# First attention layer of a two-layer graph network: an order written out by hand on all engines, with fixed distances

## The chip, the cores and the metric

The kernel runs on one core of a Trainium2 chip. The core has five engines, each with its own queue that is worked through in order: TensorE (PE; its weight loads are shown apart as PEld), VectorE (DVE), ScalarE (ACT), GpSimd (POOL) and SyncE (SP). In this kernel POOL issues the gathers from device memory and SP issues nearly all other transfers. The metric is the time of one execution on the device in microseconds (us), lower is better. Of the kernel before there are 25 timed executions (median 4665.8, from 4651.89 to 4680.75) and one profiled execution of 4664.45.

## The reference

There are 6250 nodes with 256 features each and 100,000 edges, sorted by destination; each edge has one of 6 types. A node's row is normalized, and then two attention layers follow. The change is in the first. Cut to what matters there:

```python
k_rel = einsum('nhd,rhde->rnhe', k, rel_att)      # 4 heads of 64
v_rel = einsum('nhd,rhde->rnhe', v, rel_msg)
key_e = k_rel[edge_type, edge_src]
val_e = v_rel[edge_type, edge_src]
att = (q[edge_dst] * key_e).sum(-1) * rel_pri[edge_type] / sqrt(64)
seg = edge_dst * 6 + edge_type
ex = exp(att - segment_max(att, seg)[seg])
w = ex / segment_sum(ex, seg)[seg]
hsum = segment_sum(w[:, :, None] * val_e, seg)
```

So each edge needs a gathered row (its key and its value, 512 floats), a dot product per head with the query of its destination, a softmax over the edges with the same destination and type, and a weighted sum of values into its destination.

## The kernel before, in words

An earlier part of the kernel sorts the edges by (destination, type), computes all queries into an SBUF tile `QA` (one block of 126 nodes after another) and all keys and values into a table `kv_d` in device memory. The second layer and two stages over the nodes come later and are not touched.

The first attention layer works on 832 tiles of 128 edges, in 26 chunks of 32 tiles (`C` = 32, `NC` = 26). For a tile `t` it does this:

- **Gather** (line 642, POOL): the 128 rows of key and value go into a ring of 12 lanes with 6 slots each (lines 665 to 679). `gather_more` issues the gather of tile `t` only when tile `t - 12` has been scored and tile `t - 60` has been weighed.
- **Expand q** (lines 724 to 750): SP fetches the row numbers of 4 tiles (`near`), DVE makes one-hot matrices of them (`nbe`), and PE multiplies the one-hots with a block of `QA`. The result for two tiles, `qe`, lies in PSUM with two buffers. The block number is loaded into registers of PE, 8 tiles at a time.
- **Score** (lines 753 and 756, DVE): multiply `qe` with the gathered keys (`pr`), and reduce to 4 numbers per edge (`att`). Two tiles go through one instruction.
- **Softmax over the chunk** (`chain`, from line 763 to 868): a serial string of some 20 steps that passes between PE (transposes), ACT (copies, exponentials) and DVE (forward and backward scans): the maximum of each segment first, then the sum. It ends with the weights `wt` (line 862) and, for a segment that goes on from the chunk before, a correction `factor` (line 868).
- **Weigh** (lines 892 and 897, ACT): scale the gathered values with `wt`, four instructions per tile, into `wrows` (two buffers of 4 tiles).
- **Sum** (`one_hots` line 875, product line 960, `add` line 905): DVE makes one-hots `ebn` of 4 tiles, PE multiplies them with `wrows` into `aps` (PSUM, three buffers), and DVE adds `aps` to a block of `QA`. A block's sums lie where the queries of the block before were.
- **Move** (lines 916 to 940): between two chunks the running sum of a segment that goes on is corrected with `factor`, through a product (line 929), `moved` (lines 932 and 938) and an add (line 940).

While chunk `c` is weighed and summed (`bulk(c)`), chunk `c + 1` is scored and its softmax done (`chain(c + 1)`); the loop at the end of the stage interleaves the two generators. The order in which the program is written is not the order of the queues, however. A scheduler of the framework goes over what was written and orders each engine's queue by its own estimate of when an instruction can start. In the queues that it made, the product of one tile often stands between the two products of the next q, two `pr` may come before their two reductions, adds of line 905 stand between the steps of the softmax, and some instructions of the next chunk's scoring stand among the softmax of this one.

Of the kernel before, what the change touches and what calls it, by code (L numbers as in the profile page):

```python
# [17 lines left out]
P = 128  # L18
# [6 lines left out]
def kernel(  # L25
# [81 lines left out]
    def dap(t, offset, ap):  # L107
        a = t[:, :]
        return bass.AP(tensor=a.tensor, offset=a.offset + offset, ap=ap)
# [540 lines left out]
    with ExitStack() as st:  # L650
# [13 lines left out]
        def slot(t):  # L664
            return L - 1 - (t // NL) % L
# [35 lines left out]
        def flat(v, back):  # L701
            v = v.rearrange("p h t -> p (h t)")
            return v[:, ::-1] if back else v

        def chain(c, res):

            keeps = cp.tile([P, 2, P], F32, name="keeps", bufs=2)
# [8 lines left out]
            whole_s = cp.tile([1, 2, H, C], F32, name="whole_s")  # L716
            nc.scalar.activation(whole_s, whole, AF.Exp)
            att = cp.tile([P, H, C], F32, name="att", bufs=2)
            for k in range(0, C, 8):
                t0 = c * C + k  # L720
                oh = []
                for i in range(0, 8, GT):
                    near = op.tile([P, GT, P], BF16, name="near")
                    nc.sync.dma_start(
                        near.rearrange("p g e -> p (g e)"), dap(row_d, (t0 + i) * P, [[0, P], [1, GT * P]])
                    )
                    oh.append(op.tile([P, GT, P], F32, name="nbe"))
                    nc.vector.tensor_scalar(oh[-1], near, ipart, None, op0=OP.is_equal)
                _, bs = nc.values_load_multi_w_load_instructions(
                    blk[0:1, t0 : t0 + 8],  # L730
                    engines=[mybir.EngineType.PE],
                    min_val=0,
                    max_val=NB - 1,
                    skip_runtime_bounds_check_because="blk is at most NB - 1",
                )
                for j in range(0, 8, 2):
                    t = t0 + j
                    qe = pq.tile([P, 2, D], F32, name="qe")
                    for i in range(2):
                        ordered(  # L740
                            nc.tensor.matmul(  # L741
                                qe[:, i, :],
                                oh[j // GT][:, j % GT + i, :],
                                QA[:, 1:, :D][:, bass.ds(bs[j + i], 1), :].rearrange("p a d -> p (a d)"),
                                start=True,
                                stop=True,
                            ),
                            "q",
                            "sums",
                        )  # L750
                    pr = wp.tile([P, 2, H, DK], F32, name="pr")
                    lane = t % NL
                    nc.vector.tensor_tensor(  # L753
                        pr.rearrange("p t h e -> p t (h e)"), ring[:, lane : lane + 2, slot(t), :], qe, op=OP.mult
                    )
                    nc.vector.tensor_reduce(  # L756
                        att[:, :, k + j : k + j + 2].rearrange("p h t -> p t h"), pr, AX.X, OP.add
                    )
                    scored[0] = t + 2
                    gather_more()  # L760
                    yield
            x = pt.tile([P, P], F32, name="turn")
            nc.tensor.transpose(x, att.rearrange("p h t -> p (h t)"), ident)
            yield
# [103 lines left out]
                nc.scalar.activation(factor, fps, AF.Identity, bias=ones[:, 0:1])  # L868
                res["factor"] = factor

        state = {"hot": None, "regs": {}}

        def one_hots(t):
            o = wp.tile([P, GT, P], F32, name="ebn")
            nc.vector.tensor_tensor(
                o,
                ifree[:, None, :].to_broadcast([P, GT, P]),
                dl0[:, t : t + GT, None].to_broadcast([P, GT, P]),
                op=OP.is_equal,
            )  # L880
            return o

        def bulk(c, w, factor):

            wvs, sums = {}, {}
            hot = {}

            def weigh(j):
                t = c * C + j
                if j % GT == 0:  # L890
                    wvs[j // GT] = wp.tile([P, GT, AV], F32, name="wrows")
                    nc.scalar.copy(wvs[j // GT][:, :, D:], start[:, t : t + GT, :])  # L892
                wv = wvs[j // GT]
                v = ring[:, t % NL, slot(t) + 1, :]
                for h in range(H):
                    cols = slice(h * DK, (h + 1) * DK)
                    nc.scalar.activation(wv[:, j % GT, cols], v[:, cols], AF.Copy, scale=w[:, h, j : j + 1])  # L897
                used[0] = t + 1
                gather_more()

            def add(j):
                t = c * C + j
                a = QA[:, bass.ds(state["regs"][t], 1), :].rearrange("p a d -> p (a d)")
                ordered(
                    nc.vector.scalar_tensor_tensor(a, a, same[:, t : t + 1], sums.pop(j), op0=OP.mult, op1=OP.add),  # L905
                    "sums",
                    "q",
                )
                del state["regs"][t]

            weigh(0)
            weigh(1)
            hot[0] = one_hots(c * C)
            if c:
                t = c * C - 1
                _, (at,) = nc.values_load_multi_w_load_instructions(
                    blk[0:1, t : t + 1],
                    engines=[mybir.EngineType.PE, mybir.EngineType.DVE],
                    min_val=0,
                    max_val=NB - 1,  # L920
                    skip_runtime_bounds_check_because="blk is at most NB - 1",
                )
                move = wp.tile([P, P], F32, name="move", bufs=1)
                nc.vector.tensor_scalar(
                    move, ifree, target[:, c : c + 1], top_row, op0=OP.is_equal, op1=OP.mult
                )
                a = QA[:, bass.ds(at, 1), :].rearrange("p a d -> p (a d)")
                ps = pp.tile([P, AV], F32, name="aps")
                nc.tensor.matmul(ps, move, a, start=True, stop=True)
                yield  # L930
                moved = wp.tile([P, AV], F32, name="moved", bufs=1)
                nc.vector.tensor_tensor(
                    moved[:, :D].rearrange("p (h e) -> p h e", h=H),
                    ps[:, :D].rearrange("p (h e) -> p h e", h=H),
                    factor[:, :, None].to_broadcast([P, H, DK]),
                    op=OP.mult,
                )
                nc.scalar.copy(moved[:, D:], ps[:, D:])
                ordered(
                    nc.vector.scalar_tensor_tensor(a, a, keep, moved, op0=OP.mult, op1=OP.add), "sums", "q"  # L940
                )
                yield
            for j in range(C):
                t = c * C + j
                if j % 8 == 0:
                    _, bs = nc.values_load_multi_w_load_instructions(
                        blk[0:1, t : t + 8],
                        engines=[mybir.EngineType.DVE],
                        min_val=0,
                        max_val=NB - 1,  # L950
                        skip_runtime_bounds_check_because="blk is at most NB - 1",
                    )
                    for i in range(8):
                        state["regs"][t + i] = bs[i]
                if j + 2 < C:
                    weigh(j + 2)
                if j % GT == 2 and j + 2 < C:
                    hot[j // GT + 1] = one_hots(t + 2)
                ps = sums[j] = pp.tile([P, AV], F32, name="aps")
                nc.tensor.matmul(  # L960
                    ps, hot[j // GT][:, j % GT, :], wvs[j // GT][:, j % GT, :], start=True, stop=True
                )
                if j % 8 != 0 and j:
                    add(j - 1)
                if j % 8 == 7:
                    add(j)
                yield

        res = {}
        gather_more()  # L970
        for _ in chain(0, res):
            pass
        for c in range(NC):
            todo = bulk(c, res["w"], res.get("factor"))
            ahead = chain(c + 1, res) if c + 1 < NC else iter(())
            for k in range(C // 2):
                next(ahead, None)
                if k in (1, 3) or k % 2 and k > 4:
                    next(todo, None)
            for _ in todo:  # L980
                next(ahead, None)
            for _ in ahead:
                pass

    acc0 = QA[:, :NB, :]
    adst = pers.tile([P, NB, 3, 2 * H], BF16, name="adst")
# [422 lines left out]
```

## Time and profile before

| | us |
|---|---|
| profiled execution, its own time | 4664.45 |
| its span (first to last instruction) | 4662.7 |
| median of 25 timed executions | 4665.8 |
| first `pr` of the first attention layer | 943.4 |
| transposes of the scores (line 763) of chunks 0, 1 and 25 | 993.0, 1041.3, 2628.3 |
| last add of the layer (line 905) | 2683.4 |

The page gives busy time by engine, the span in 40 slices, a chain of waits, and groups of instructions by line. A group's line has its count, its busy time and the mean of one in ns, and after the bar the idle time of its engine just before it with what ended it. "remote" there means that a signal arrived without an instruction or transfer that ended just then; "issue" that nothing shown ended the wait. Timeline rows give start and length in us, the engine, line and operation, how many were merged (x2), and in brackets the idle time before. A length of two merged instructions that is under twice the length of one shows that they overlap: what counts for a sum is the distance of starts. An fp32 product is recorded as two weight loads and two matmuls, so 832 products of a line are x1664.

### The profile page before, as it was taken

How to read it: one execution, taken by the hardware profiler on the slowest of the kernel's cores; microseconds unless marked ns; L12 is line 12 of the kernel's file. 1: busy time of each engine (PE TensorE's matmuls, PEld its weight loads, DVE VectorE, ACT ScalarE, POOL GpSimd, SP SyncE). 2: the span in 40 equal slices, each digit the busy share in tenths (PEclk: the TensorE clock that was granted, in tenths of full speed). 3: DMA queues.
4: the chain of work that ended last, by engine and by line, in shares of the span. 5: the costliest groups of instructions: out<-in, count | busy, mean ns of one | idle time of the engine just before them, and what ended most of it. 6: DMA issues, size and time to landing. Idle time of an engine off the chain costs nothing. (4 is left out here: it accounts for less than half of the span.)

```text
span 4662.7 us, 51896 instructions
## 1 busy us (share of the span) xinstructions
PE 3113.7 (67%) x12464; PEld 2112.4 (45%) x12464; DVE 3049.0 (65%) x7131; ACT 1448.7 (31%) x5577; POOL 1722.9 (37%) x1808
## 2 busy tenths in 40 slices
PE   4996699856676666666666788852566665666672
PEld 3775577634444444444444455531333443344432
DVE  7567211057777777767776788862666666666798
ACT  4332233225554555545544722210100100000102
POOL 0000000064444544454444200025676766676500
PEclk9998899977778887878887988865777777767676
DMA  2334333264445544454454332323333333334423
GB/s 91 122 115 117 84 128 117 104 201 134 140 144 156 160 145 139 133 158 136 132 152 147 68 85 73 72 78 108 100 106 114 111 109 113 107 111 115 82 69 101
DMA packets 265355, 545.35 MB, mean 117 GB/s; under 512 B 66696, under 2 KB 175227, under 8 KB 255483
## 3 DMA queue, kind: packets, MB, share of 16 engines
q0 software_dynamic: 106496, 328.97, 25.2%
q1 hardware_dynamic: 150929, 208.18, 14.6%
q10 hardware_dynamic: 7636, 4.88, 0.4%
q8 instruction: 111, 1.82, 0.2%
q14 instruction: 183, 1.50, 0.1%
HBM read 436.56 MB, written 105.28 MB: 116 GB/s over the span
## 5 line engine op out<-in xcount | busy, mean ns | idle before, releaser
L642 POOL DMA_INDIRECT ring<-kv_d,idx x832 | 811.3, 975 | 947.0 <-ACT wrows L897 425.2
L642 POOL DMA_INDIRECT rows<-xw_d,idx x832 | 871.7, 1048 | 477.2 <-issue 357.0
L1288 PE MATMUL aps<-wrows,ebn 128*128 128x264 f32 x1664 | 665.5, 541 | 290.5 <-DVE acc L1296 164.2
L897 ACT ACTIVATE wrows<-ring,wt 128x64 f32<-128x64 f32 x3328 | 833.7, 335 | 6.1 <-issue 5.9
L960 PE MATMUL aps<-wrows,ebn 128*128 128x258 f32 x1664 | 601.6, 470 | 253.0 <-DVE QA L905 105.5
L741 PE MATMUL qe<-QA,nbe 128*128 x1664 | 537.6, 461 | 212.1 <-DVE pr L753 78.2
L1288 PEld LDWEIGHTS aps<-wrows,ebn 128*128 128x128 f32 x1664 | 384.1, 258 | 507.7 <-issue 229.6
L741 PEld LDWEIGHTS qe<-QA,nbe 128*128 128x128 f32 x1664 | 369.6, 232 | 335.8 <-issue 170.0
L960 PEld LDWEIGHTS aps<-wrows,ebn 128*128 128x128 f32 x1664 | 333.6, 225 | 408.8 <-ACT wrows L897 167.6
L753 DVE TENSOR_TENSOR pr<-ring,qe 128x512 f32<-128x512 f32 x416 | 279.0, 680 | 296.6 <-remote 189.7
L171 POOL MEMSET ntype<- 128x128 int32 x100 | 29.7, 298 | 1148.7 <-DVE hm L186 768.8
L905 DVE SCALAR_TENSOR_TENSOR QA<-QA,same,aps 128x258 f32 x832 | 389.7, 468 | 83.2 <-PE aps L960 48.6
L1296 DVE TENSOR_TENSOR acc<-acc,aps 128x264 f32 x832 | 349.5, 420 | 43.9 <-issue 12.6
L1152 ACT COPY asr<-rows 128x16 f32<-128x16 f32 x208 | 44.8, 218 | 792.2 <-DMA rows<-xw_d,idx 772.2
L1272 DVE TENSOR_TENSOR wrows<-rows,ex 128x1024 f32<-128x1024 f32 x208 | 253.9, 1221 | 47.5 <-PE aps L1288 19.2
L756 DVE TENSOR_REDUCE att<-pr 128x8 f32<-128x512 f32 x416 | 272.4, 678 | 0.6
L892 ACT CAST wrows<-start 128x8 f32<-128x8 bf16 x208 | 39.2, 189 | 606.0 <-remote 232.5
L344 ACT COPY rel<-nps 128x384 f32<-128x384 f32 x400 | 163.2, 493 | 96.3 <-PE nps L343 96.3
L195 PE MATMUL nps<-wa_s,tm 128*128 128x256 f32 x600 | 167.6, 438 | 6.0 <-DVE tm L186 6.0
L1180 DVE TENSOR_TENSOR ad<-ad 128x256 f32<-128x256 f32 x26 | 11.0, 424 | 241.8 <-ACT ad L1177 135.1
L334 PE MATMUL nps<-hm,wv_s 128*128 128x128 f32 x1200 | 160.5, 284 | 0.0
L334 PE MATMUL nps<-hm,wk_s 128*128 128x128 f32 x1200 | 160.5, 284 | 0.0
(368 smaller groups left out, 4503.5 us busy)
## 6 DMA issues: line engine op xcount, KB each, us to landing
kv_d<-rel SPq DMA_DIRECT2D x49, 1512.0 KB
near<-row_d SPq DMA_DIRECT2D x208, 128.0 KB
nbe<-row_d SPq DMA_DIRECT2D x26, 1024.0 KB
ring<-kv_d,idx POOLq DMA_INDIRECT x832
rows<-xw_d,idx POOLq DMA_INDIRECT x832
xbuf<-in_x_dram SPq DMA_DIRECT2D x98, 126.0 KB
xw_d<-xw SPq DMA_DIRECT2D x49, 128.0 KB
xbuf<-xw_d SPq DMA_DIRECT2D x49, 128.0 KB
```

Of the source, the lines that this page charges most:

```text
L195: nc.tensor.matmul(ps, m[:, t, c, :], W[:, t, c, :], start=(t == 0 and c == 0), stop=False)
L334: nc.tensor.matmul(tp[:, o, :], W[:, t, c, cols], m[:, t, c, :], start=(t == 0 and c == 0), stop=False)
L642: nc.gpsimd.indirect_dma_start(out=to, out_offset=None, in_=table[:, :], in_offset=bass.IndirectOffsetOnAxis(ap=index, axis=0))
L741: nc.tensor.matmul(qe[:, i, :], oh[j // GT][:, j % GT + i, :], QA[:, 1:, :D][:, bass.ds(bs[j + i], 1), :].rearrange("p a d -> p (a d)"), s ...
L753: nc.vector.tensor_tensor(pr.rearrange("p t h e -> p t (h e)"), ring[:, lane : lane + 2, slot(t), :], qe, op=OP.mult)
L756: nc.vector.tensor_reduce(att[:, :, k + j : k + j + 2].rearrange("p h t -> p t h"), pr, AX.X, OP.add)
L897: nc.scalar.activation(wv[:, j % GT, cols], v[:, cols], AF.Copy, scale=w[:, h, j : j + 1])
L905: nc.vector.scalar_tensor_tensor(a, a, same[:, t : t + 1], sums.pop(j), op0=OP.mult, op1=OP.add),
L960: nc.tensor.matmul(ps, hot[j // GT][:, j % GT, :], wvs[j // GT][:, j % GT, :], start=True, stop=True)
L1272: nc.vector.tensor_tensor(wv[:, :, :, :DK], rows[:, :, :, :DK], ex[:, 0, mine, :, None].to_broadcast([P, GT, H, DK]), op=OP.mult,)
L1288: nc.tensor.matmul(ps.rearrange("p h e -> p (h e)"), oh[:, j, :], wv[:, j].rearrange("p h e -> p (h e)"), start=True, stop=True,)
L1296: nc.vector.tensor_tensor(a, a, ps, op=OP.add)
```

## The change

The whole layer is now recorded under `manual_schedule`: every engine's queue has its instructions in the order in which they are written, and the scheduler moves nothing there. The order is written anew to that end:

- The row numbers are fetched two groups of 4 tiles ahead (`fetch_rows`), the one-hots for q made one group ahead (`near_one_hots`), the products for q issued one pair of tiles ahead (`expand_q(t + 2)` before `score(t)`), also across a chunk's end.
- The add of a tile comes after the next tile's product, throughout, also across groups of 8 tiles and across a chunk's end (`add(t - 1)` after `multiply(t)`). Before, the adds of the 7th and 8th tile of each group of 8 both came right after the 8th product.
- The one-hots for the sums (`one_hots`) are made after the second tile of a group of 4 for the next group, also across chunks.
- In the loop over a chunk's 16 scored pairs, the first three pairs go with the move (three steps), and each of the other 13 pairs with one tile's sum. The remaining 19 tiles go one by one with the steps of the softmax.
- The softmax of the first chunk is done before any other work of the layer starts.

No instruction is added to or taken from the work on a tile, and no buffer's size is changed. The diff, cut to its core:

```diff
+        def near_one_hots(g):
+            if g < NT // GT:
+                near_hot[g] = op.tile([P, GT, P], F32, name="nbe")
+                nc.vector.tensor_scalar(near_hot[g], nears.pop(g), ipart, None, op0=OP.is_equal)
+                fetch_rows(g + 2)
+
+        def expand_q(t):
...
+            qe = spread[t] = pq.tile([P, 2, D], F32, name="qe")
+            for i in range(2):
+                ordered(
+                    nc.tensor.matmul(
+                        qe[:, i, :],
+                        near_hot[t // GT][:, t % GT + i, :],
+                        QA[:, 1:, :D][:, bass.ds(pe_regs.pop(t + i), 1), :].rearrange("p a d -> p (a d)"),
...
+        def score(t, to):
+            if t % GT == 0:
+                near_one_hots(t // GT + 1)
+            pr = wp.tile([P, 2, H, DK], F32, name="pr")
...
+            scored[0] = t + 2
+            gather_more()
...
         def chain(c, res):
...
-            for k in range(0, C, 8):
...
+            for t in range(c * C, (c + 1) * C, 2):
+                expand_q(t + 2)
+                score(t, att[:, :, t % C : t % C + 2])
+                yield
...
         def bulk(c, w, factor):
...
-            weigh(0)
-            weigh(1)
-            hot[0] = one_hots(c * C)
+            for j in range(2):
+                weigh(c * C + j, w)
             if c:
+                add(c * C - 1)
...
             for j in range(C):
                 t = c * C + j
...
                 if j + 2 < C:
-                    weigh(j + 2)
-                if j % GT == 2 and j + 2 < C:
-                    hot[j // GT + 1] = one_hots(t + 2)
-                ps = sums[j] = pp.tile([P, AV], F32, name="aps")
-                nc.tensor.matmul(
-                    ps, hot[j // GT][:, j % GT, :], wvs[j // GT][:, j % GT, :], start=True, stop=True
-                )
-                if j % 8 != 0 and j:
-                    add(j - 1)
-                if j % 8 == 7:
-                    add(j)
+                    weigh(t + 2, w)
+                if j % GT == 1:
+                    one_hots(t // GT + 1)
+                multiply(t)
+                if j:
+                    add(t - 1)
                 yield
 
         res = {}
-        gather_more()
-        for _ in chain(0, res):
-            pass
-        for c in range(NC):
-            todo = bulk(c, res["w"], res.get("factor"))
-            ahead = chain(c + 1, res) if c + 1 < NC else iter(())
-            for k in range(C // 2):
-                next(ahead, None)
-                if k in (1, 3) or k % 2 and k > 4:
-                    next(todo, None)
-            for _ in todo:
-                next(ahead, None)
-            for _ in ahead:
-                pass
+        with tc.manual_schedule():
+            gather_more()
+            for g in range(2):
+                fetch_rows(g)
+            near_one_hots(0)
+            for g in range(1):
+                one_hots(g)
+            expand_q(0)
+            for _ in chain(0, res):
+                pass
+            for c in range(NC):
+                todo = bulk(c, res["w"], res.get("factor"))
+                ahead = chain(c + 1, res) if c + 1 < NC else iter(())
+                early = 3 if c else 0
+                for k in range(C // 2):
+                    next(ahead, None)
+                    if k < early or k >= 3:
+                        next(todo, None)
+                for _ in todo:
+                    next(ahead, None)
+                for _ in ahead:
+                    pass
+            add(NT - 1)
```

## The prediction

> **What bounds the kernel now.** I read the page first, for the share of this layer; then busy time by stage, cut where the transposes of the scores (line 763) stand; then VectorE's waits in the long stage; then timelines, for what one instruction costs from its start to the next one's.
>
> The page:
>
> ```profile
> span 4662.7 us, 51896 instructions
> L642 POOL DMA_INDIRECT ring<-kv_d,idx x832 | 811.3, 975 | 947.0 <-ACT wrows L897 425.2
> L753 DVE TENSOR_TENSOR pr<-ring,qe 128x512 f32<-128x512 f32 x416 | 279.0, 680 | 296.6 <-remote 189.7
> ```
>
> The sum is made against the profiled execution, 4664.45 (its span and 1.75 around it); the median of 25 is 4665.8, 1.4 above, so nothing is corrected for it. The multiplication with q stood idle longer than it worked, mostly on a signal with no visible releaser.
>
> Busy time by stage (length, then PE, PEld, DVE, ACT, POOL, granted clock, DMA share, GB/s):
>
> ```profile
> 1041.00:2628.00 1587.00, 1036.37 (x3445) 694.97 (x3443) 1174.32 (x2635) 832.29 (x3641) 740.98 (x759) 0.81 0.49 144
> 2628.00:2649.00 21.00, 17.52 (x56) 9.57 (x54) 19.17 (x54) 17.00 (x76) 0.00 (x0) 0.84 0.00 1
> 2649.00:2684.00 35.00, 24.73 (x73) 12.15 (x72) 22.71 (x47) 33.03 (x144) 1.31 (x2) 0.95 0.01 3
> ```
>
> The first row is 24 periods, each with one chunk's sum and the next one's scoring and softmax: 1587 / 24 = 66.1 us. DVE is busy 1174.32 / 24 = 48.9 of that, more than any other engine, and idle 17.2. The second row is the softmax of the last chunk beside sums, with nothing left to gather: DVE is busy 91%. So DVE bounds the layer, and 17.2 us a period are all that a better order can win. What DVE waits for in the first row (total, times, longest):
>
> ```profile
> DVE pr L753 <- remote: 160.3, 36, 8.4
> DVE pr L753 <- PE qe L741: 48.5, 51, 3.6
> DVE QA L905 <- PE aps L960: 37.8, 61, 2.0
> DVE one L774 <- issue: 36.2, 10, 6.2
> DVE pr L753 <- issue: 33.2, 29, 5.7
> DVE QA L905 <- remote: 12.8, 7, 3.2
> ```
>
> Two kinds. In 48.5 + 37.8 = 86.3 us (3.6 a period) PE was really late. In 160.3 + 36.2 + 33.2 + 12.8 = 242.5 us (10.1 a period) PE had ended long before. One such place, PE first, then DVE:
>
> ```profile
> 1477.92 3.39 PE L741 MATMUL qe<-QA,nbe 128*128 x8
> 1488.87 2.08 PE L741 MATMUL qe<-QA,nbe 128*128 x4 [7.13 <-DVE pr L753]
> ```
>
> ```profile
> 1478.08 0.69 DVE L875 TENSOR_TENSOR ebn<-ifree,dl 128x512 f32<-128x512 f32 x1
> 1478.68 0.48 DVE L905 SCALAR_TENSOR_TENSOR QA<-QA,same,aps 128x258 f32 x1
> ...
> 1488.13 0.69 DVE L753 TENSOR_TENSOR pr<-ring,qe 128x512 f32<-128x512 f32 x1 [6.64 <-remote]
> ...
> 1495.35 0.50 DVE L728 TENSOR_SCALAR nbe<-near,ipart 128x512 f32<-128x512 bf16 x1
> 1495.77 1.27 DVE L753 TENSOR_TENSOR pr<-ring,qe 128x512 f32<-128x512 f32 x2
> 1496.96 1.27 DVE L756 TENSOR_REDUCE att<-pr 128x8 f32<-128x512 f32 x2
> 1498.15 0.47 DVE L905 SCALAR_TENSOR_TENSOR QA<-QA,same,aps 128x258 f32 x1
> 1498.54 0.68 DVE L753 TENSOR_TENSOR pr<-ring,qe 128x512 f32<-128x512 f32 x1
> ```
>
> The products for q ended at 1481.3, the `pr` that needs them starts at 1488.13, and then PE too has been idle for 7.13. I call these **held signals**. None appears before the layer's first gather, nor in the second row above, where POOL is idle; I take them to belong to long trains of gathers. What holds them the trace doesn't tell.
>
> **The change, part by part.** The second timeline also gives what an instruction costs in a full queue, start to start: `pr` (1496.96 − 1495.77) / 2 = 0.60, reduction 0.60, add 0.39, `nbe` 0.42 at most (0.40 elsewhere), `ebn` 0.60. No instruction on a tile is added or removed, so the change is worth what it does to the 17.2 idle us.
>
> *First half of a period* (16 pairs scored; the move; 13 tiles summed). On DVE: 16 × (0.60 + 0.60) = 19.2; 8 `nbe` × 0.40 = 3.2; 13 adds × 0.39 = 5.1 (12 of this chunk, one left over); 3 `ebn` × 0.60 = 1.8; `move`, `moved` and the move's add about 1.0 as their busy times; loading block numbers 0.1 (no busy time is shown for it; a gap, by estimate). Sum **30.4**. The others' cover: ACT weighs a tile in 1.0 (33.03 us for 144 instructions, four a tile and some others, in the third row), against 1.9 of DVE per step; PE has a pair for q and one product.
>
> *POOL* gathers the same 832 tiles in the same sequence, a pair 2 × 1.25 = 2.5 (record 0.975, starts 1.25 apart), more than DVE's 1.9. The first half thus eats 16 × 0.6 = 9.6 us, 8 tiles, of the 12 tiles' lead; the softmax half, in which nothing is scored, gives it back. Should the lead run out, `pr` waits for gathers; before, that cost 12.8 us in the whole stage.
>
> *Softmax half* (19 tiles, each beside a step of the softmax). The second row is the same mixture: **21.0**. Bounds: its busy 19.17 below; above, ACT's weighing, 19 × 1.0, and the softmax's own copies and exponentials, 2.5, make 21.5. At its end the next chunk need not wait: the first pair's q is already expanded, and weighing runs two tiles ahead.
>
> *q two tiles ahead, adds one tile behind* (lines 741, 753, 905, 960). These lengthen PE's head start by a step, about 1.9 us, against true lateness of 48.5 / 51 = 1.0 and 37.8 / 61 = 0.6 us a time. I take 1.0 of the 3.6 us a period as left; bounds 0 and 3.6. What is late next is the other direction: `qe` has two PSUM buffers, so the products for pair t + 2 wait on PE for the `pr` of t − 2, and the tile's product for the sum is queued behind them. In steady state that `pr` is a step old; after a DVE stall both catch up together.
>
> *One-hots four tiles ahead* (lines 728, 875). They move to fixed places, same count. `near` is fetched two groups ahead, four steps or some 7.7 us, and in before its one-hots waited for it 1.0 us in the whole stage. Cost 0; without that cover, the 2.4 us in which a gather lands (from POOL's record to its end) bound one such wait, 8 a period at worst.
>
> *SP.* 208 `near` and, per chunk, the loads of `keeps` and `whole` are the same transfers. The latter now stand behind a chunk's last `near`, and `whole` waits for the scans (line 790) of the chunk before, some 5 us into the softmax half. It is needed 25 us later and the next `near` some 15 later: 0, or 2 us a period if it should land late.
>
> *Edge.* The first softmax now stands alone: in before, from 993 to 1014, `pr` of chunk 1 ran between its steps. Of the work moved out, about half filled idle DVE; I take **+6** once (0 to 12). The last chunk is as before.
>
> *Held signals.* They hit whoever waits for PE, and two tiles of distance (about 2 us) do not cover 6.6. The number of gathers per period is the same, so I keep **10.1**. Bounds: 0 (second row: none), and doubled, 20, since the first half is now one unbroken train and a strict order has nothing else to run.
>
> **Sum:** 30.4 + 21.0 + 1.0 + 10.1 = 62.5 a period against 66.1: 24 × 3.6 = 86 less; 4664.45 − 86 + 6 = **4584**. Its own range, with 0 to 3.6 for true lateness, ± 1.5 for the halves: 4540 to 4640.
>
> *A rule that speaks against this.* After idling 7.13 us, PE takes 2.08 for four matmuls, where eight took 3.39, and the granted clock of the stage is 0.81. The Trainium skill ("TensorE: Matmul & The Clock Gate", section "HAM oscillation — how this bites in real kernels") says that PE idling longer than some 3.4 us falls back to half clock. By it, any wait of a strictly ordered PE behind DVE would be paid twice. If PE ran at half clock through the whole first half (8 matmuls in 3.39, so 1.7 per pair, and 1.1 for a tile's product), its step of 2.8 would pass DVE's 1.9: 13 × 0.9 = 12 us a period, and 4872 in all. By the rows, PE idles that long only in a held signal, once or twice a period, and its cost is in the 10.1.
>
> **The rivals.**
>
> *Held signals vanish.* If they came from the particular order in before (matmul after matmul with waits between), the period is 52.4: 24 × 13.7 = 329 less, **4341**. For it: 2628 to 2649 runs so. Against it: that stretch has no gathers. Chance 0.16.
>
> *Held signals grow: slower.* Place: every `pr` of the first half, with PE's product and DVE's add queued behind it. From 66.1 − 52.4 − 0.25 (the edge) = **13.5** us a period on, the change loses. For it: the trains get longer, and when before stalled, adds and softmax steps of other tiles could sometimes run ahead. Against it: in before, too, each queue was fixed once compiled, and `pr` stood at the head of it. At 16 us: 68.4, 24 × 2.3 + 6 = 61 more, 4726; at 20: 24 × 6.3 + 6 = 157 more, 4822. As one number **4740**. Chance 0.28.
>
> *Nothing comes of it:* the removed PE waits return as waits for PSUM or for gathers (the lead of 12 runs out: 2 to 4 us a period). Then 4664 ± 20. Chance 0.12: 0.04 faster, 0.05 same, 0.03 slower.
>
> **How the numbers follow.** The forecast has 0.44. Faster: 0.44 + 0.16 + 0.04 = 0.64; same 0.05; slower 0.28 + 0.03 = 0.31. About 0.2%, 9 us, is what a measurement of this kernel can tell from no change. The range reaches to 4420, leaving out two thirds of the case with no held signals, and to 4745, leaving out four tenths of the slower one (0.11 each, with the tails).
>
> **What would show it.** Right: line 782 of the new kernel (the transposes) 62 to 63 us apart; first halves near 31 plus held time, softmax halves near 21; `pr <- PE qe` and `QA <- PE aps` together under 30 us; "remote" and "issue" still near 240. Wrong: softmax halves of 25 or more (the interleaving is bound by ACT or by a step of the string); `pr <- DMA ring` in tens of us (gather lead too short); "remote" below 100 or above 350 (held signals follow the order, not the gathers).

## The result and the profile after

The changed kernel takes 4729.35 us (median of 7 runs, 4720.96 to 4738.47) against 4665.69 for the kernel before: a ratio of 1.0136, 95% interval 1.0119 to 1.0152. It is slower by 64 us where 82 us of gain were forecast. The profiled execution of the changed kernel took 4723.66, its span is 4721.9.

The page of the changed kernel; the last two lines are groups (count, busy time and mean, and after the bar the idle time before them with what ended most of it):

```profile
span 4721.9 us, 51320 instructions
L642 POOL DMA_INDIRECT ring<-kv_d,idx x832 | 812.9, 977 | 1003.5 <-issue 376.8
L756 DVE TENSOR_TENSOR pr<-ring,qe 128x512 f32<-128x512 f32 x416 | 283.4, 681 | 298.1 <-remote 228.5
```

The idle time before `pr` is what it was (298.1, before 296.6), and more of it is "remote". The transposes of the scores of chunks 1 and 25 (line 782) stand at 1049.5 and 2688.2, so 24 periods take 1639 us, 68.3 each (66.1 before). Busy time by stage; the columns are window, length, then PE, PEld, DVE, ACT, POOL, the granted clock, DMA share and GB/s:

```profile
1049.00:2688.00 1639.00, 1070.88 (x3453) 696.32 (x3452) 1233.71 (x2640) 833.28 (x3648) 742.89 (x759) 0.82 0.47 140
```

DVE now works 51.4 us a period (48.9 before) and is idle 16.9 (17.2 before). What DVE waits for in these 24 periods (total, times, longest):

```profile
DVE pr L756 <- remote: 214.5, 51, 6.9
DVE QA L934 <- PE aps L929: 43.2, 46, 3.5
DVE QA L934 <- issue: 23.7, 14, 3.5
DVE pr L756 <- PE aps L929: 16.5, 12, 2.0
DVE QA L934 <- remote: 14.8, 8, 2.8
DVE pr L756 <- PE qe L738: 14.7, 26, 0.6
DVE QA L934 <- PE qe L738: 12.9, 9, 2.1
DVE pr L756 <- issue: 12.6, 4, 4.0
```

The order did in part what it was meant to do: a `pr` waits 14.7 us for its own products where it had waited 48.5, but an add waits 43.2 us for its product (37.8 before). The four rows of held signals, "remote" and "issue", are 265.6 us (242.5 before; 273.6 if the first and the last chunk are counted too, the number that two expectations below start from), and the four rows of waits for PE are 87.3. A stretch of DVE's timeline in a scored half:

```profile
1495.23 0.47 DVE L934 SCALAR_TENSOR_TENSOR QA<-QA,same,aps 128x258 f32 x1
1495.62 0.68 DVE L756 TENSOR_TENSOR pr<-ring,qe 128x512 f32<-128x512 f32 x1
1496.34 0.69 DVE L759 TENSOR_REDUCE att<-pr 128x8 f32<-128x512 f32 x1
1496.94 0.47 DVE L934 SCALAR_TENSOR_TENSOR QA<-QA,same,aps 128x258 f32 x1
1497.33 0.48 DVE L718 TENSOR_SCALAR nbe<-near,ipart 128x512 f32<-128x512 bf16 x1
1503.90 0.69 DVE L756 TENSOR_TENSOR pr<-ring,qe 128x512 f32<-128x512 f32 x1 [6.09 <-remote]
```

Two things are in it. A step runs as reckoned, about 2 us, until a signal is held for 6.09 (the profile models when a product ends on PE, so it can't tell whether the signal or the end of the product was late). And `pr` to its own reduction is 1496.34 − 1495.62 = 0.72, not 0.60; the reduction reads what `pr` has just written. By halves, averaged over 24 periods: the softmax half, transposes to `wt`, takes 22.3 (reckoned 21.0), the scored half 45.9 (reckoned 30.4 and the held time).

### The profile page after: what moved, and what is told of

It is laid out like the page before. It is cut to its first block, busy times and chain, and to the rows that moved or that the text cites. A ratio compares the mean times of both kernels' runs of the same rounds, so it can differ in the third digit from the quotient of the medians.

```text
span 4721.9 us, 51320 instructions
## 1 busy us (share of the span) xinstructions
PE 3152.1 (67%) x12464; PEld 2116.5 (45%) x12464; DVE 3111.3 (66%) x7131; ACT 1447.9 (31%) x5577; POOL 1728.0 (37%) x1808
## 5 line engine op out<-in xcount | busy, mean ns | idle before, releaser
L1313 PE MATMUL aps<-wrows,ebn 128*128 128x264 f32 x1664 | 676.4, 549 | 282.6 <-DVE acc L1321 176.1
L738 PE MATMUL qe<-QA,nbe 128*128 x1664 | 571.6, 483 | 374.2 <-DVE pr L756 247.2
L929 PE MATMUL aps<-wrows,ebn 128*128 128x258 f32 x1664 | 586.4, 452 | 76.6 <-issue 26.7
L756 DVE TENSOR_TENSOR pr<-ring,qe 128x512 f32<-128x512 f32 x416 | 283.4, 681 | 298.1 <-remote 228.5
L934 DVE SCALAR_TENSOR_TENSOR QA<-QA,same,aps 128x258 f32 x832 | 394.2, 474 | 128.2 <-PE aps L929 54.3
L759 DVE TENSOR_REDUCE att<-pr 128x8 f32<-128x512 f32 x416 | 286.1, 688 | 14.4
L1193 PE MATMUL ad<-adst,nbe 128*128 x832 | 102.6, 179 | 92.6 <-issue 82.2
```

The costliest lines, as they stand in the source:

```text
L738: nc.tensor.matmul(qe[:, i, :], near_hot[t // GT][:, t % GT + i, :], QA[:, 1:, :D][:, bass.ds(pe_regs.pop(t + i), 1), :].rearrange("p a d ...
L756: nc.vector.tensor_tensor(pr.rearrange("p t h e -> p t (h e)"), ring[:, lane : lane + 2, slot(t), :], spread.pop(t), op=OP.mult)
L759: nc.vector.tensor_reduce(to.rearrange("p h t -> p t h"), pr, AX.X, OP.add)
L929: nc.tensor.matmul(sums[t], hots[t // GT][:, t % GT, :], wvs[t // GT][:, t % GT, :], start=True, stop=True)
L1313: nc.tensor.matmul(ps.rearrange("p h e -> p (h e)"), oh[:, j, :], wv[:, j].rearrange("p h e -> p (h e)"), start=True, stop=True,)
```

## The experiments

Theories. **G**: signals are held by gathers (later **T** or **R**: by long trains of them, at full rate); **O**: by the strict order. **D**: the fixed order costs DVE time, because dependent instructions stand side by side. **H**: DVE's step does not bound the scored half.

One fact is needed for the numbers. The kernel before was run again on each occasion, and took 4716, 4726 and 4665 us on three of them but 4312 and 4314 on the last two. The ratios are to the kernel before of the same occasion. What the last two show comes below.

### Without the gathers

Both kernels, and later two relatives, with one edit (line numbers move by one or a few):

```diff
-                gather(
+                if t < NL * L:
+                    gather(
```

> The changed kernel with only the first 72 of 832 gathers of the layer issued (the ring is filled once; later tiles use stale rows, so 760 gathers of the work are left out). All else stands. Theory G (signals are held by trains of gathers): the 'remote' and 'issue' waits of DVE, 273.6 us in the changed kernel, go almost entirely: 4729 - 260 = about 4470. Theory O (they follow from the strict order, whatever is gathered): over 4680, with 'remote' and 'issue' still above 200 us.

> The kernel before with the same 760 gathers left out. Theory G: 'remote' and 'issue' waits, 242.5 us, go: about 4666 - 230 = 4435. What the two orders cost without held signals is then compared: by the prediction's own sum the fixed order should be faster by some 80 us here; theory D (the fixed order puts instructions that depend on each other side by side on DVE, 0.72 from pr to its reduction where 0.60 was counted, 0.58 from add to add where 0.39 was) has the fixed order slower or equal here too, by 0 to 60 us.

Measured on one occasion: the changed kernel 4406.44, ratio 0.9351 (0.9329 to 0.9373); the kernel before 4369.16, 0.9272 (0.925 to 0.9294). The 24 periods of the changed kernel, then of the kernel before:

```profile
1047.00:2338.00 1291.00, 964.20 (x3452) 605.61 (x3451) 1218.64 (x2639) 835.01 (x3648) 0.00 (x0) 0.94 0.08 23
```

```profile
1042.00:2308.00 1266.00, 971.89 (x3442) 657.39 (x3441) 1160.79 (x2634) 830.30 (x3637) 0.00 (x0) 0.89 0.08 23
```

A period is 53.8 in the changed kernel and 52.8 in the kernel before, every period of the changed one between 53.5 and 54.3, and no "remote" wait is left in either. G holds and O falls, and more time went than G had said (4470 and 4435 were expected). So gathers and what comes with them cost 68.3 − 53.8 = 14.5 us a period in the changed kernel and 66.1 − 52.8 = 13.3 in the kernel before, not the 10.1 that the prediction read off the rows. (The periods with gathers are from the first profiles; on the occasion of these runs the kernel before took 51 us more, so held time itself moves by up to 2 us a period.) The granted clock fits an explanation of the rest by slower work of PE, though no run separates it: 0.81 and 0.82 with gathers, 0.89 and 0.94 without (rows of PE after a held signal stand below, beside the clock rule).

D also has the sign here: with nothing held, the fixed order is 37 us slower, where the prediction's sum has it 80 faster. DVE works 1218.64 us in its 24 periods, in the other order 1160.79.

### The new text under the scheduler

```diff
-        with tc.manual_schedule():
+        if True:
```

> The changed kernel's text, but the scheduler orders the queues again. If the loss comes from the queues being held to the written order (theory D, or a strict order that can't go around a late signal): back near the kernel before, 4650 to 4690. If it comes from what the new text does in any order (the first softmax alone, one-hots and q made earlier, loads of keeps late): it stays at 4710 to 4740.

4657.25, ratio 0.9887 (0.9856 to 0.9917): not back at the kernel before, but slightly faster than it, which neither reading had. So the new text in the scheduler's order gains 1.1%, and in the strict order it loses 1.4% (each against the kernel before of its own occasion). Without gathers the same text was run too:

> The changed kernel's text under the scheduler, with only the first 72 of 832 gathers (760 left out; stale rows). If the new text saves DVE or PE time of its own in the scheduler's order: under 0.925 (the kernel before so: 0.927; the changed one: 0.935). If its 1.1% was only that signals were held less: 0.925 to 0.93.

4186.33, ratio 0.9712 on one of the two late occasions, so that the ratio says nothing beside 0.927. Its trace says more: 24 periods of 49.2 us, against 52.8 and 53.8 of the two kernels without gathers. By this, taken on different occasions, the new text saves 3.6 us a period in the scheduler's order.

### The dependent neighbours

```diff
             scored[0] = t + 2
             gather_more()
+            yield
+            nc.vector.tensor_reduce(to.rearrange("p h t -> p t h"), pr, AX.X, OP.add)
```

(and the reduction after `pr` taken out.)

> The changed kernel with one thing moved: the reduction of a pair stands behind the tile's one-hots and add instead of right behind its pr. Theory D: pr to next instruction falls from 0.72 to 0.60, 16 times a period: 25 x 16 x 0.12 = 48 us less, about 4681. Theory H (DVE's step is not what bounds the scored half; PE's held signals or POOL's 2.5 us per pair are): the time saved is waited, 4715 to 4735.

4794.19, ratio 1.0173 (1.0147 to 1.0198): no gain over 1.0136; D's 0.01 is not seen. The times that were expected can't be compared, as the kernel before took 4716 us on this occasion and not 4666; the ratio is what H says, that the time saved is waited, or a little worse. Without gathers:

> The changed kernel with only the first 72 gathers and with the reduction of a pair behind the tile's add. Theory D (dependent neighbours on DVE are what the fixed order costs): 25 x 13 x 0.12 = 39 us under the changed kernel without gathers (0.9351), 0.927. If something else bounds the scored half: 0.933 to 0.937.

4272.41, ratio 0.9907, again on a late occasion, so the periods are compared: 52.6 us against 53.8. `pr` to the add takes 0.60, and the reduction follows 0.39 after that. 1.2 us a period, 30 us in all, answer to D's 39, by two occasions. So D is right about DVE, and while signals are held the late reduction gains nothing.

### What in the gathers holds the signals

Four kernels on one occasion: a pause on POOL after each gather; a longer one after every sixth; half the length of a row; half the rows.

```diff
                     ring[:, t % NL, slot(t) : slot(t) + 2, :].rearrange("p a d -> p (a d)"), kv_d, idx[:, t, 0:1]
                 )
+                nc.gpsimd.memset(rest, 0.0)
```

```diff
+                if t % 6 == 5:
+                    for _ in range(3):
+                        nc.gpsimd.memset(rest, 0.0)
```

```diff
+                    gather(
+                        ring[:, t % NL, slot(t), :], kv_d[:, :].rearrange("a (two d) -> (a two) d", two=2), idx[:, t, 0:1]
+                    )
```

```diff
+                n = P if t < NL * L else P // 2
```

> The changed kernel with a memset of 128x384 on POOL behind every gather (some 0.4 us), so that gathers start about 1.65 us apart and not 1.25. As ratios to the kernel before (the changed kernel has 1.0136). Theory T (a train of more than about 8 gathers at full rate holds the signals): most of the 11.4 held us a period go, the period falls from 68 to 56 or 58, ratio 0.94 to 0.96. Theory B (it is what is gathered, not its rate): the held time stays, and POOL's 53 us a period are added to the pressure: 1.01 to 1.04.

> The changed kernel with three memsets of 128x1024 on POOL behind every sixth gather (some 2.9 us), so that no train is longer than 7.5 us. Theory T: ratio 0.94 to 0.96, as a train ends before signals begin to be held (they began 9 us after a train's start in the traces). Theory B: 1.01 to 1.04.

> The changed kernel, from the 73rd gather on with rows of 256 floats instead of 512 (the table read as twice as many rows of half the length, so rows and values are not the right ones): the same 128 rows per gather, half the bytes. Theory B (bytes): the held time falls to half or less, ratio 0.93 to 0.985. Theory N (number of rows or of gathers): ratio 1.005 to 1.02, held waits still above 220 us.

> The changed kernel, from the 73rd gather on with 64 rows of 512 floats instead of 128 (the other half of the tile keeps stale rows): half the bytes and half the rows, the same number of gathers. If e7 leaves the held time and this one takes it away, it goes with the number of rows; if both leave it, with the number of gathers (ratio about 1.01); if both take it away, with the bytes (0.93 to 0.97).

| | us | ratio | interval |
|---|---|---|---|
| pause after each gather | 4524.81 | 0.9573 | 0.9546 to 0.9599 |
| pause after every sixth | 4605.73 | 0.9754 | 0.9738 to 0.977 |
| rows of 256 floats | 4611.34 | 0.9756 | 0.9735 to 0.9777 |
| 64 rows | 4797.19 | 1.0156 | 1.0128 to 1.0184 |

A pause of 0.43 us, with the same gathers and bytes, makes the kernel 4.3% faster than the kernel before, with all its work done. POOL and DVE's largest waits there:

```profile
1490.52 0.43 POOL L678 MEMSET rest<- 128x384 f32 x1
1491.12 0.95 POOL L642 DMA_INDIRECT ring<-kv_d,idx  x1 [0.16 <-ACT wrows L913]
1492.07 0.43 POOL L678 MEMSET rest<- 128x384 f32 x1
```

```profile
DVE pr L758 <- DMA ring<-kv_d,idx: 81.8, 58, 2.6
DVE QA L936 <- PE aps L931: 12.9, 30, 0.6
```

"remote" has gone, and in its place is what the prediction feared of the lead of 12 tiles: waits for gathers, 81.8 us. The period is 58.7, between the 53.8 without gathers and the 68.3 with them at full rate. With the pause after every sixth gather "remote" is gone too, and `pr` waits 101.9 us for gathers; 0.9754 is therefore outside both expected ranges. T holds for what holds the signals. Bytes alone are not it: the "remote" and "issue" rows of `pr` and the adds in 24 periods are 303.7 us with half the rows, started 1.21 us apart, against 265.6 in the changed kernel, but 123.7 with rows of half the length. The two have the same packets (48 a gather, some 131 KB). Which property of a row matters stays open.

Gathers that land late are not what the held signals are. By the packets of the gathers' queue, the last one of a gather comes 3.6 us (median) after the gather's start in the changed kernel and 3.8 in the same kernel where nothing is held (below); with half the rows it comes after 2.4, and signals are held all the same.

How much of a pause is needed, and does it work in the old order:

> The changed kernel with a memset of 128x64 behind every gather: POOL was idle 0.30 between two gathers and 0.16 before one that follows a memset, so that gathers stay about 1.25 to 1.30 apart. Theory R (the rate of gathers holds the signals): little changes, ratio to the kernel before 0.99 to 1.015. Theory S (it is enough that POOL does anything else between two gathers): 0.935 to 0.96.

> The changed kernel with a memset of 128x224 behind every gather: gathers some 1.4 apart, 45 us a period. Theory R with its edge below 1.4: no held signals, and POOL's wait is shorter than with 128x384 (81.8 us of waits for gathers there): a period of 55 to 56, ratio 0.935 to 0.95. With its edge above 1.4: held signals come back in part, 0.96 to 1.0.

> The kernel before with the same memset of 128x224 behind every gather. Theory D (the fixed order costs DVE time by itself, as the 37 us between the two kernels without gathers say): 0.005 to 0.012 lower than the changed kernel with that pause. If the fixed order's distances pay once nothing is held, as the prediction reckoned: 0.005 to 0.018 higher than it.

> The changed kernel with the memset of 128x224 and with the reduction of a pair behind the tile's add. Theory D: with nothing held, 0.12 us for each of some 13 pairs a period show, 25 x 13 x 0.12 = 39 us, 0.008 lower than with the memset alone. If POOL bounds the scored half then: the same within 0.003.

| | us | ratio | interval |
|---|---|---|---|
| memset of 128x64, starts 1.28 apart | 4727.37 | 1.0113 | 1.0062 to 1.0165 |
| memset of 128x224, 1.42 apart | 4483.23 | 0.9588 | 0.9536 to 0.9639 |
| kernel before, memset of 128x224 | 4724.79 | 1.0129 | 1.0079 to 1.0178 |
| reduction late, memset of 128x224 | 4491.77 | 0.9623 | 0.9572 to 0.9675 |

It is the rate (R) and not that something stands between (S). The memset of 128x224 lands just between R's two ranges: its period is 59.2, and 22.1 us of "remote" are left at the adds. The kernel before doesn't gain, but not for the reason that was weighed: the scheduler moved the memsets away from the gathers, into POOL's waits:

```profile
1510.23 1.67 POOL L678 MEMSET rest<- 128x224 f32 x5
...
1517.00 1.28 POOL L642 DMA_INDIRECT ring<-kv_d,idx  x1 [0.32 <-issue]
1518.58 0.95 POOL L642 DMA_INDIRECT ring<-kv_d,idx  x1 [0.31 <-issue]
1519.83 0.95 POOL L642 DMA_INDIRECT ring<-kv_d,idx  x1 [0.30 <-issue]
```

Its "remote" wait at `pr` is still 122.4 us, and `pr` waits 135.1 for gathers (12.8 in the kernel before). So this run could not compare the orders. The late reduction again brings nothing beside the same pause: waits for gathers grow from 30.7 to 61.1 us.

### The same kernels where nothing is held

To tie the pause to its gather, the memset was put into the lane that the gather fills:

```diff
+                to = ring[:, t % NL, slot(t) : slot(t) + 2, :].rearrange("p a d -> p (a d)")
+                nc.gpsimd.memset(to[:, :384], 0.0)
+                gather(to, kv_d, idx[:, t, 0:1])
```

> The kernel before with a memset of 384 columns of the very ring lane that the gather then fills, so that the scheduler must keep it ahead of that gather (some 1.6 us a gather on average, in pairs). Theory R (the rate of gathers holds the signals, in any order): no held signals, and POOL's 53 us a period or DVE's 51 to 55 bound it: 0.95 to 0.97, like the changed kernel with its pause (0.957). If the fixed order was what let the pause work there: 0.99 to 1.02.

> The changed kernel's text under the scheduler with the same tied memset of 384 columns. Theory R: 0.945 to 0.965. If the fixed order was what let the pause work: 0.98 to 1.0.

> The changed kernel as it is. In a session with held signals (the kernel before at 4650 to 4730): 1.011 to 1.017, as first measured. In one without (before near 4312): theory D, 37 us by the runs without gathers, 1.006 to 1.013; the prediction's sum without held signals would have it at 0.98 to 1.0.

> The new text under the scheduler with the tied memset of 384 columns. In a session with held signals, theory R: they go, and the time is near the 4326 us measured in the session without, plus what the second layer holds (which has no pause): 0.93 to 0.955. If the pause needs the fixed order: 0.98 to 1.0. In a session without: 1.003 again.

| | us | before | ratio | interval |
|---|---|---|---|---|
| kernel before, tied pause | 4422.02 | 4312.49 | 1.0253 | 1.0231 to 1.0276 |
| new text, scheduler, tied pause | 4325.78 | 4312.49 | 1.003 | 1.002 to 1.0039 |
| the changed kernel | 4316.34 | 4314.4 | 0.9998 | 0.9988 to 1.0009 |
| new text, scheduler, tied pause | 4328.48 | 4314.4 | 1.0034 | 1.0021 to 1.0047 |

On these two occasions signals were not held: no trace taken then has a "remote" wait of DVE in the layer. So the pause could only cost time (2.5% in the kernel before), and R could not be tested in the scheduler's order. With the same tied pause and on the same occasion, the new text under the scheduler is 96 us faster than the kernel before. The scheduler's rows have no partner without a pause, so what the pause costs there isn't known. The third row is the one that counts: the same kernel, the same gathers 1.25 us apart, and it ties with the kernel before. Its 24 periods, and DVE's largest waits in them:

```profile
1028.00:2331.00 1303.00, 967.25 (x3453) 609.84 (x3453) 1222.36 (x2640) 834.61 (x3648) 750.50 (x764) 0.94 0.61 176
```

```profile
DVE pr L756 <- PE qe L738: 14.0, 27, 0.6
DVE QA L934 <- PE aps L929: 11.3, 26, 0.8
DVE pr L756 <- DMA ring<-kv_d,idx: 6.7, 6, 1.9
```

A period is 54.3, DVE is busy 94%, no "remote" is left. Both expectations for this case were off or at their edge: it is no loss of 0.006 to 0.013 (D), and 0.98 to 1.0 (the prediction's sum) only just. So the loss of 1.36% is there only with held signals. Without gathers the fixed order lost 37 us and here it loses none; what makes that up isn't shown, as there is no profile of the kernel before from that occasion. So how the 64 us divide between the order by itself and held signals stays open: the runs without gathers have 1.0 us a period for the order and 1.2 for held signals, this run nothing for the order.

Nor do the runs show why signals are held on some occasions and not on others. It is not the chip alone: one chip took 4716 us for the kernel before on one occasion and 4312 on another. The traces show one more difference. Of the landing signals of the 1664 gathers of both layers (16 each, 26624), the trace of the changed kernel has 8477 where signals are held and 26571 where they are not; of PE's signals from 950 to 2300 us it has 81% and all, and before 900 us all in both. So on some occasions, while gathers run, signals merge or go missing in the record. This is not the same as a held signal: with the pause after each gather 14890 are there, and none is held. Whether both have one cause, and whether the recording itself plays a part, no run shows.

Why the fixed order is hit harder isn't shown either. A count of the trains fits in part. If gathers that start within 0.6 us of the end of the one before are one train, 29% of the layer's gathers in the kernel before are the ninth or later of their train, 39% in the changed kernel (whose softmax half scores nothing, so that POOL runs through the scored half), and 25% under the scheduler with the new text: the sequence of their ratios. But the kernel with 64 rows has 32% and is no faster than the changed kernel, and the changed kernel on the occasion where nothing is held has 74%. The length of the trains alone is not enough.

## Why the prediction was wrong

The chosen forecast (4584) was wrong in sign; the rival "held signals grow" had the place and, at 16 us a period, the number (4726 against 4729), at a chance of 0.28. That the number is so close is partly luck: its 52.4 and 16 measured 53.8 and 14.5. Its reason, longer trains, is not shown. By the steps:

- **First half, 30.4.** 33.0 where nothing is held. The largest term missing is the dependence: 16 × 0.12 = 1.9 us for `pr` to its reduction; PE's lateness below, 1.05, accounts for the rest. The prediction took 0.60 from a place where two `pr` come before two reductions, and used it for a `pr` that its reduction follows. The trace of before had the right pair, directly after the held signal that the prediction showed, 0.72 apart:

```profile
1488.13 0.69 DVE L753 TENSOR_TENSOR pr<-ring,qe 128x512 f32<-128x512 f32 x1 [6.64 <-remote]
1488.85 0.69 DVE L756 TENSOR_REDUCE att<-pr 128x8 f32<-128x512 f32 x1
```

- **Softmax half, 21.0.** 21.3 where nothing is held: right.
- **True lateness of PE, 1.0.** 14.0 + 11.3 = 25.3 us in 24 periods, 1.05, where nothing is held: right. In the forecast's own case 87.3 us are left (57.9 in the two rows that were to be under 30). As they are 25 where nothing is held, the rest goes with held signals; that it is PE's slow work after them is argued from the rows below.
- **POOL's lead, one-hots, SP.** Waits for gathers 6.7 us in 24 periods where nothing is held: cover as reckoned.
- **Edge, +6.** The first transposes of chunk 1 come 8.2 later (1049.5 against 1041.3), with held signals in it: right in size.
- **Held signals, 10.1 in both orders.** This is the step that failed. By the runs without gathers they and the gathers cost 13.3 in the kernel before and 14.5 in the changed one; in the changed one the gathers by themselves are 0.5 of it (54.3 where nothing is held, against 53.8). The rows "remote" and "issue" count the wait itself (11.1 a period in the changed kernel), but not the waits for PE behind it or its slower work.

The sum with the measured terms: (53.8 + 14.5 − 62.5) × 24 = 139, and 4584 + 139 = 4723, the profiled 4723.66; 53.8 and 14.5 add up to the measured period by their definition, so this shows the shares and proves nothing more. So 1.4 of the 5.8 us a period is the base, and 4.4 the held time. The same mistake made the gain: 66.1 − 10.1 left 56.0 for the kernel before without held signals, and the new order's 52.4 looked better by 3.6; the run without gathers says 52.8.

The forecast's own range was also narrower than its terms: true lateness from 0 to 3.6 and ± 1.5 for the halves, added up, give 4524 to 4682 and not 4540 to 4640. The measured time lies outside both.

The rule on the clock that was weighed there: PE's timeline in the changed kernel has a pair's products right after a held signal, and 10 us later:

```profile
1504.65 2.08 PE L738 MATMUL qe<-QA,nbe 128*128 x4 [6.72 <-DVE pr L756]
...
1515.07 1.13 PE L738 MATMUL qe<-QA,nbe 128*128 x4
```

They take 2.08 and then 1.13 us, and the granted clock of the stage is 0.82 with held signals and 0.94 without. That is the direction of the rule in the Trainium skill ("TensorE: Matmul & The Clock Gate", section "HAM oscillation — how this bites in real kernels"), by which PE falls to half clock when it idles too long; the extreme case, half clock through all of the scored half (4872), didn't come. That case was priced with 1.7 us for a pair's products; by these rows it is 2.08.

## What to carry to other kernels

Before an order is priced, a run without the suspected transfers tells what the order costs by itself. The waits in the profile understated what a recurring stall cost here (10.1 and 11.1 us a period against 13.3 and 14.5). A distance of one or two steps covers lateness of that size and nothing longer: if stalls are three times as long, look at what causes them (here the rate of one engine's gathers) and not at the order of the rest. A reduction right behind the multiplication that it reads started 0.72 us after it, an independent instruction 0.60, so start distances have to be taken from the same pair of neighbours. And the kernel before belongs in every comparison: it moved by some 8% between occasions, six times the effect of the change.

## What was not expected of the hardware

- With gathers of 128 rows of 2 KB, started 1.25 us apart in long trains, DVE waited for PE up to 9 us (9.1 in the new text under the scheduler, 8.4 in the kernel before) on most occasions; 1.28 apart it still did (ratio 1.0113), 1.42 apart much less (0.9588; 22.1 us of "remote" left at the adds), 1.55 apart not at all. A memset of 0.43 us that computes nothing made the changed kernel 4.3% faster than the kernel before.
- With 64 rows at a time signals were held as much as with 128 (303.7 us against 265.6).
- On two of the five occasions of the experiments nothing was held at all, and the kernel before took 4312 and 4314 us and not 4665 to 4726. There the tied pause cost the kernel before 2.5%. The gain of the pause was measured in the changed kernel alone, and only where the kernel before took 4665 to 4726.
- A pause written as an instruction of its own was moved by the scheduler to where POOL is idle; under the fixed order it stayed where it was put.
